# Making layer 3's masks on VectorE in the last two graphs, with the whole instruction order searched anew

## The chip, the cores and the metric

The kernel runs on one NeuronCore of a Trainium2 chip. A core has five engines that run side by side, each in the order in which its instructions were issued: TensorE (PE in the profile, with PEld for its weight loads), VectorE (DVE), ScalarE (ACT), GpSimd (POOL), and SyncE (SP), which here only issues DMAs. The metric is the device time of one execution in microseconds (us), the median over several executions. Everything is in fp32, except the masks of layer 3, which are int8.

## The reference

Four graph layers in a row are applied to each of B = 16 graphs of N = 1024 nodes with D = 128 features. `adj` is a 1024 x 1024 matrix per graph, with about 1.5% of its entries and the diagonal above zero. Each layer adds its output to `x`.

```
# before every layer: h = max(layernorm(x), 0);   x = x + layer(h)
layer 0, three times: h = h @ W + b;  n = h / |h|;  h = (adj * (n n^T)) @ h;  relu but for the last
layer 1: y = relu(((1 + eps) h + adj^T h) @ W1 + b1) @ W2 + b2, masked by node
layer 2: h = h @ W;  attn = softmax(where(adj > 0, tanh(s1_i + s2_j), -1e15));  attn @ h
layer 3: h = h @ W^T + b;  e = (h A) h^T;  e = e + e^T
         att = softmax(where(adj > 0, e, 0), axis=1) * adj
         h' = relu(att @ h);  three sigmoid gates of [x, h'];  o * tanh(sigmoid(i h' + f x))
```

The part that changes is `where(adj > 0, e, 0)` in layer 3: it needs a 0/1 mask of `adj > 0`.

## The kernel before, in words

A graph is held as eight row blocks of 128 nodes. `turn` brings `adj` in transposed, as eight tiles `adjT` of 128 x 1024 (`aT[j]`); layers 0, 2 and 3 use them. Layer 1 loads `adj` once more as it is (`adjL`).

Layers 0 and 3 need a symmetric 1024 x 1024 product. The class `Square` computes the blocks on and above the diagonal by matmul (tile `sq`, L789). The blocks below are mirrors: in the graphs from 1 to B-3 half of them take a way over HBM (`above`, `by_hbm`, `got`), in the first and the last two graphs all of them are turned by TensorE (L799) from a copy that ScalarE makes of the upper blocks (`keep`, L821). `accumulate` (L851) and `accumulate_nodes` (L862) hold the matmuls that sum over the eight rows.

Layer 3 runs over the rows j = 0 to 7. For each row:

1. the mask: ScalarE takes `Sign` of `aT[j]` into an int8 tile (L1249) and `Relu` of that in place (L1251). It needs only `adjT`, so it can be made long before the row; there are five mask buffers.
2. VectorE multiplies mask and product and keeps the row maximum (L1260, twice 512 columns, with a small read of the accumulator each), and a small reduction joins the two maxima (`top`, L1281).
3. ScalarE takes the exponential with its sum (L1292), VectorE the reciprocal (`sum`, L1306) and the product with `aT[j]` (L1301, twice 512). In the last two graphs GpSimd makes that product for four of the odd rows (L1297).
4. ScalarE scales a block of h (`hs`, L1310), and TensorE accumulates (L851).

Layer 2 has for each row a tanh (L1174) and an exp (L1178) on ScalarE, a masked product on VectorE (L1182) and the accumulation (L862). A layer norm ends with `hn` (L727 on VectorE, L734 on ScalarE); its turned copy `hnT`, and layer 3's `gT` and `h3T`, leave PSUM by ScalarE (L651).

The order of all instructions, DMAs too, is fixed while the kernel is built. The class `Plan` collects every operation with an estimated duration, reads and writes. `order` is a list scheduler: it takes, of the operations that can start on the engine that is free first, the one with the lowest rank. The rank is the due time of the graph, less the estimated work behind the operation, less a lead from the table `LEADS`. A key of `LEADS` names layer, engine and tile, and may end in an edge: ` <0` and ` <1` for the first two graphs, ` >1` and ` >0` for the last but one and the last; inner graphs have none. So a lead moves one kind of operation earlier or later against all others. `KINDS` says for each kind of tile which pool it takes buffers from, how many may be held in all and how many of these by graphs younger than the oldest unfinished one. `PERIOD` and `LAST` set the due times. Up to three graphs are in work at once.

```
o.rank = (self.deadline(o.batch) - o.tail - lead, o.seq)
...
"chunk": ("big", 11, 4)          # tile kind: (pool, most in all, most of younger graphs)
```

[...]

Of the kernel before, what the change touches and what calls it, by code (L numbers as in the profile page):

```python
# [11 lines left out]
AF = mybir.ActivationFunctionType  # L12
ALU = mybir.AluOpType
# [211 lines left out]
def tile_adj_preln(  # L225
# [40 lines left out]
    FLAGS = set("CabcdkxhyzTGmrHW")  # L266
# [61 lines left out]
    for load_it in first:  # L328
# [13 lines left out]
        "adjT": ("adjT", 16, 16), "adjL": ("adjL", 5, 5), "x": ("x", 3, 3), "w4": ("big", 9, 10),  # L342
        "chunk": ("big", 11, 4), "above": ("above", 2, 1), "got": ("got", 1, 1), "ps": ("bank", 6, 8),
        "acc": ("bank", 8, 8), "small": ("small", 8, 9), "row": ("row", 3, 2), "hbm": ("hbm", 3, 3),
        "hrow": ("hrow", 1, 2), "mask": ("mask", 5, 5), "dot": ("dot", 8, 5),
    }
    PERIOD, LAST, AHEAD, WINDOW = 59, 45.5, 2, 0.05

    LEADS = {
        "T DMA raw": 123, "T PE raw": -181.5, "T ACT adjT": 61.5, "T DVE su": 140.5, "x DMA x": -64.5,  # L350
        "0 DVE st": -1445.5, "0 DVE mv": -195, "0 POOL rstd": -141.5, "0 DVE nb": -665.5, "0 DVE hn": -152,
        "0 ACT hn": -103.5, "0 PE ps": -501, "0 ACT hT": -310, "00 PE psP": 544.5, "00 DVE h": -430.5,
        "00 PE ps": -551, "00 ACT hTn": -805, "00 ACT sq": -172.5, "00 DVE ss": 414, "00 POOL rn": 411.5,
        "00 PE sq": 2, "00 ACT above": 104.5, "00 DVE ew": 336, "00 PE acc0": -2325.5, "00 POOL params": 20.5,
        "00 DMA params": 82.5, "00 DVE params": -360, "00 PE params": -157.5, "00 ACT hT": 355.5,
        "01 PE psP": 156.5, "01 DVE h": 139.5, "01 PE ps": 225, "01 ACT hTn": -125.5, "01 ACT sq": -32.5,
        "01 DVE ss": -67.5, "01 POOL rn": -35, "01 PE sq": 593, "01 ACT above": 635, "01 DVE ew": 275,
        "01 PE acc0": -359, "01 ACT hT": -478.5, "02 PE psP": -84.5, "02 DVE h": -107, "02 PE ps": 47.5,
        "02 ACT hTn": -775.5, "02 ACT sq": -143.5, "02 DVE ss": -254.5, "02 POOL rn": 110, "02 PE sq": 1342.5,
        "02 ACT above": 29, "02 DVE ew": -245.5, "02 PE acc0": 217.5, "02 DVE x": 285, "T DMA adjT": 560,  # L360
        "T DVE adjT": -431, "1 DVE st": -145, "1 DVE mv": 965, "1 POOL rstd": 26, "1 DVE nb": 533.5,
        "1 DVE hn": 337, "1 ACT hn": 218, "1 DVE x": 944, "1 DMA adjL": -492, "1 DVE adjL": -518.5,
        "1 PE acc1": 300.5, "1 ACT g": -18, "1 PE py": -994.5, "1 ACT y1": -259.5, "1 PE py2": -40,
        "2 DVE st": 0.5, "2 DVE mv": 798, "2 POOL rstd": 84.5, "2 DVE nb": 219, "2 DVE hn": 39.5,
        "2 ACT hn": 285, "2 PE ps": -196, "2 ACT hnT": 91.5, "2 DVE alone": -149, "2 DVE x": -82.5,
        "2 PE psP": -261.5, "2 ACT h": -7, "2 DVE hrow": -299, "2 PE pf": -86, "2 ACT hfl": 3.5,
        "2 PE pt": -280.5, "2 ACT sr": 11, "2 DMA sd": -11.5, "2 DMA s1": -14.5, "2 DVE h": 147,
        "2 ACT e2": -31.5, "2 DVE e2": 44, "2 PE acc2": 764.5, "2 DVE rden": 64.5, "3 DVE st": 146.5,
        "3 DVE mv": 86.5, "3 POOL rstd": 69.5, "3 DVE nb": 1010.5, "3 DVE hn": -14.5, "3 ACT hn": 108,
        "3 PE ps": 521, "3 ACT hnT": 308, "3 PE pg": -9.5, "3 ACT gT": 17, "3 PE psP": 420.5, "3 DVE h": 402,  # L370
        "3 ACT h3T": 139.5, "3 ACT mask": -48, "3 PE sq": 515, "3 ACT above": 311, "3 DVE e3": -455.5,
        "3 DVE top": -226, "3 ACT e3": 428.5, "3 DVE sum": -301.5, "3 ACT hs": 1350.5, "3 PE acc3": -603.5,
        "3 ACT hpT": 260.5, "3 PE psN": 363, "3 ACT hp": 80.5, "3 DVE gate": -98, "3 ACT gate": 331,
        "3 POOL z": 77.5, "3 DVE z": -1081.5, "3 ACT z": 200, "3 DMA z": -878.5, "00 DVE above": 0,
        "00 DMA by": -38, "00 DMA got": 94, "01 DVE above": 266.5, "01 DMA by": -11.5, "01 DMA got": -343.5,
        "02 DVE above": 345, "02 DMA by": -362, "02 DMA got": 262.5, "3 DVE above": 240.5, "3 DMA by": 0,
        "3 DMA got": -727, "3 POOL e3": -253, "3 POOL hp": -418, "2 PE p1": -128.5, "2 ACT s1": -60,
        "T DMA raw <0": -220, "T PE raw <0": 37, "T ACT adjT <0": 8, "T DVE su <0": 268, "x DMA x <0": 168,
        "0 DVE st <0": -20, "0 DVE mv <0": -925.5, "0 POOL rstd <0": -219, "0 DVE nb <0": -16.5,
        "0 DVE hn <0": -172.5, "0 ACT hn <0": -463, "0 PE ps <0": 280.5, "0 ACT hT <0": 245.5,  # L380
        "00 PE psP <0": 16, "00 DVE h <0": 79, "00 PE ps <0": -40.5, "00 ACT hTn <0": 110.5,
        "00 ACT sq <0": 231, "00 DVE ss <0": -47, "00 POOL rn <0": 246.5, "00 PE sq <0": 67,
        "00 ACT above <0": 319.5, "00 DVE ew <0": -499.5, "00 PE acc0 <0": -127, "00 POOL params <0": -154,
        "00 DMA params <0": -52.5, "00 DVE params <0": -1.5, "00 PE params <0": 147.5, "00 ACT hT <0": -7.5,
        "01 PE psP <0": 245, "01 DVE h <0": 321.5, "01 PE ps <0": -35, "01 ACT hTn <0": 50.5,
        "01 ACT sq <0": 207.5, "01 DVE ss <0": -82, "01 POOL rn <0": -229.5, "01 PE sq <0": 1050.5,
        "01 ACT above <0": -44.5, "01 DVE ew <0": -183.5, "01 PE acc0 <0": 692, "01 ACT hT <0": -89,
        "02 PE psP <0": -136, "02 DVE h <0": -203, "02 PE ps <0": 0, "02 ACT hTn <0": -39.5,
        "02 ACT sq <0": -79.5, "02 DVE ss <0": 1, "02 POOL rn <0": -25, "02 PE sq <0": 207.5,
        "02 ACT above <0": 674.5, "02 DVE ew <0": -3.5, "02 PE acc0 <0": -198, "02 DVE x <0": 615.5,  # L390
        "T DMA adjT <1": -827, "T DVE adjT <1": -472, "T ACT adjT <1": 461, "1 DVE st <0": -232,
        "1 DVE mv <0": -265.5, "1 POOL rstd <0": 0, "1 DVE nb <0": -67, "1 DVE hn <0": 133, "1 ACT hn <0": 0,
        "1 DVE x <0": 402, "1 DMA adjL <0": -1226, "1 DVE adjL <0": 170.5, "1 PE acc1 <0": 827,
        "1 ACT g <0": 322, "1 PE py <0": 155, "1 ACT y1 <0": 102.5, "1 PE py2 <0": 178.5, "2 DVE st <0": 471,
        "2 DVE mv <0": -86.5, "2 POOL rstd <0": 0, "2 DVE nb <0": 79, "2 DVE hn <0": -357,
        "2 ACT hn <0": 108.5, "2 PE ps <0": -41, "2 ACT hnT <0": 53.5, "2 DVE alone <0": -173, "2 DVE x <0": 0,
        "2 PE psP <0": 565.5, "2 ACT h <0": 127.5, "2 DVE hrow <0": 0, "2 PE pf <0": 404.5,
        "2 ACT hfl <0": -458.5, "2 PE pt <0": 29, "2 ACT sr <0": -4, "2 DMA sd <0": -177.5,
        "2 DMA s1 <0": -231.5, "2 DVE h <0": 148.5, "2 ACT e2 <0": -217, "2 DVE e2 <0": -334,
        "2 PE acc2 <0": -70, "2 DVE rden <0": -231.5, "3 DVE st <0": -264.5, "3 DVE mv <0": 112.5,  # L400
        "3 POOL rstd <0": 41.5, "3 DVE nb <0": 379.5, "3 DVE hn <0": 33.5, "3 ACT hn <0": 62.5,
        "3 PE ps <0": 28.5, "3 ACT hnT <0": 391, "3 PE pg <0": -257.5, "3 ACT gT <0": 304, "3 PE psP <0": 17,
        "3 DVE h <0": -134, "3 ACT h3T <0": 43, "3 ACT mask <0": -116, "3 PE sq <0": 137.5,
        "3 ACT above <0": 274.5, "3 DVE e3 <0": 0, "3 DVE top <0": -269, "3 ACT e3 <0": -190,
        "3 DVE sum <0": -266, "3 ACT hs <0": 119, "3 PE acc3 <0": -253.5, "3 ACT hpT <0": 52,
        "3 PE psN <0": 42, "3 ACT hp <0": 114.5, "3 DVE gate <0": -477, "3 ACT gate <0": 224,
        "3 POOL z <0": -168.5, "3 DVE z <0": 115, "3 ACT z <0": -372, "3 DMA z <0": -268, "x DMA x <1": -50,
        "0 DVE st <1": 6.5, "0 DVE mv <1": -91.5, "0 POOL rstd <1": -321.5, "0 DVE nb <1": 0,
        "0 DVE hn <1": -14, "0 ACT hn <1": 0, "0 PE ps <1": -84, "0 ACT hT <1": 489.5, "00 PE psP <1": 458,
        "00 DVE h <1": -3.5, "00 PE ps <1": -85, "00 ACT hTn <1": -11.5, "00 ACT sq <1": 89,  # L410
        "00 DVE ss <1": 304, "00 POOL rn <1": 571.5, "00 PE sq <1": -0.5, "00 ACT above <1": 133.5,
        "00 DVE ew <1": -82.5, "00 DVE above <1": 306.5, "00 PE acc0 <1": -216, "00 DMA by <1": -110.5,
        "00 DMA got <1": -25, "00 ACT hT <1": 0, "01 PE psP <1": -27, "01 DVE h <1": 266, "01 PE ps <1": -257,
# [1120 lines left out]
```

## Time and profile before

| what | value |
|---|---|
| median of 3 runs | 2431.18 us (2430.99 to 2432.51) |
| the profiled execution's own time | 2431.62 us |
| its span, first to last instruction | 2429.9 us |
| busy PE, DVE, ACT, POOL | 2393.4, 1979.3, 1504.5, 246.7 us |
| matmul records | 11905 |
| masks L1249 and L1251 | 128 each, mean 1056 and 1052 ns |

The profile is one execution. Busy time is given per engine; a wait is put down to what released the engine last. A busy PE includes modelled ends of its matmuls, so the idle time of PE is a lower bound of what it lost. PEclk is the share of full speed that was granted to TensorE's clock.

### The profile page before, as it was taken

Reading aid. Unit: us, or ns where it says so; the run is one execution under the profiler, and the core shown is the slowest. Engines: PE = TensorE matmul, PEld = TensorE weight load, DVE = VectorE, ACT = ScalarE, POOL = GpSimd, SP = SyncE. Lnnn points to the kernel's source line nnn. Section 1 sums busy time; section 2 is a strip of 40 time slices with the busy share of each in tenths; the row PEclk is TensorE's granted clock in tenths of the full one; section 3 lists DMA queues with packets and bytes.
Section 4 is the critical chain, followed back from the end, with each engine's and each line's share of the span. In section 5 each row is a group of like instructions: output and inputs, shape, how many; then the busy total and the mean of one; then the engine's idle time right before and its main releaser. Section 6 shows DMA issues by size and latency. Waiting matters only on the chain.

```text
span 2429.9 us, 35227 instructions
## 1 busy us (share of the span) xinstructions
PE 2393.4 (98%) x11905; PEld 1588.7 (65%) x11905; DVE 1979.3 (81%) x5513; ACT 1504.5 (62%) x2661; POOL 246.7 (10%) x168
## 2 busy tenths in 40 slices
PE   8999999999999999999999999999999999999987
PEld 5568566675766757576675766757666575765764
DVE  6658889887888988889887888878889887895765
ACT  7316856656575666666656576566656656673587
POOL 3000010110101010010100101110010100000112
PEclk9999999999999999999999999999999999999989
DMA  9232939568393874929658394874929638072100
GB/s 192 71 101 52 165 67 175 124 99 170 71 175 95 137 149 82 179 61 162 142 88 165 69 173 114 107 168 78 189 68 150 150 66 148 27 105 70 44 1 18
DMA packets 1103541, 271.31 MB, mean 112 GB/s; under 512 B 937224, under 2 KB 1084816, under 8 KB 1103360
## 3 DMA queue, kind: packets, MB, share of 16 engines
q1 hardware_dynamic: 1083200, 258.35, 58.8%
q10 hardware_dynamic: 19264, 9.70, 1.4%
q8 instruction: 94, 1.54, 0.3%
q0 software_dynamic: 896, 1.01, 0.3%
q14 instruction: 87, 0.71, 0.1%
HBM read 206.00 MB, written 62.98 MB: 111 GB/s over the span
## 4 chain that ended last, share of the span: by engine, by line
PE 92%; SPq 2%; DVE 2%; DMA 2%; ACT 2%; issue 0%; POOLq 0%; POOL 0%; DVEq 0%; ACTq 0%
PE acc L851 34%; PE sq L789 19%; PE acc L862 18%; PE psP L629 5%; PE sq L799 4%; PE py L1080 2%; PE py L639 2%; PE ps_hTn L598 2%; SPq L938 2%; PE psN L629 1%; PE pg L639 1%; PE ps_hnT L598 1%; DMA by_hbm<-above 1%; DMA got<-by_hbm 1%; PE ps_hT L598 1%; SPq L842 0%
## 5 line engine op out<-in xcount | busy, mean ns | idle before, releaser
L1018 DVE SCALAR_TENSOR_TENSOR ew<-sq,rn,adjT 128x512 f32<-128x512 f32 x612 | 435.4, 739 | 83.3 <-ACT above L821 57.3
L851 PE MATMUL acc<-ew,h 128*128 128x512 f32 x1024 | 475.4, 593 | 0.1
L789 PE MATMUL sq<-hTn 128*128 128x512 f32 (+3 forms) x1152 | 433.1, 489 | 0.7 <-DVE ew L1018 0.5
L821 ACT COPY above<-sq 128x256 f32<-128x256 f32 (+3 forms) x432 | 167.0, 392 | 386.6 <-PE sq L799 223.6
L789 PEld LDWEIGHTS sq<-hTn 128*128 128x128 f32 x1152 | 196.6, 191 | 147.4 <-issue 89.0
L851 PEld LDWEIGHTS acc<-ew,h 128*128 128x128 f32 x1024 | 180.2, 190 | 166.0 <-issue 139.5
L862 PEld LDWEIGHTS acc<-h,ew 128*128 128x128 f32 x2048 | 241.0, 192 | 22.5 <-issue 9.2
L862 PE MATMUL acc<-h,ew 128*128 128x128 f32 x2048 | 250.7, 275 | 0.4 <-DVE ew L1018 0.3
L851 PE MATMUL acc<-e,hs 128*128 128x512 f32 x512 | 241.0, 601 | 5.7 <-ACT hs L1310 3.2
L862 PEld LDWEIGHTS acc<-h,e 128*128 128x128 f32 x2048 | 234.0, 193 | 12.7 <-issue 9.9
L862 PE MATMUL acc<-h,e 128*128 128x129 f32 x2048 | 235.1, 276 | 5.2 <-DVE e L1182 5.2
L851 PE MATMUL acc<-adjL,hn 128*128 128x512 f32 x512 | 233.0, 593 | 0.4 <-ACT hn L755 0.4
L591 POOL TENSOR_TENSOR rstd<-ve,mhalf 128x8 f32<-128x8 f32 x64 | 105.4, 1648 | 1104.6 <-DVE ve L710 1040.1
L799 PEld LDWEIGHTS sq<-ident,above 128*128 128x128 f32 x960 | 125.9, 141 | 113.8 <-issue 90.2
L949 ACT ACTIVATE adjT<-adjT 128x1024 f32<-128x1024 f32 x120 | 126.6, 1055 | 101.8 <-DVE adjT L946 96.7
L799 PE MATMUL sq<-ident,above 128*128 128x128 f32 x960 | 175.2, 273 | 0.3 <-DVE ew L1018 0.3
L1182 DVE SCALAR_TENSOR_TENSOR e<-adjT,e 128x512 f32<-128x512 f32 x256 | 160.1, 686 | 16.2 <-ACT e L1178 16.2
L1301 DVE TENSOR_TENSOR e<-e,adjT 128x512 f32<-128x512 f32 x248 | 164.3, 691 | 3.1 <-ACT e L1292 3.0
L811 DVE STREAM_TRANSPOSE above<-sq 128x512 f32<-128x512 f32 x208 | 144.8, 705 | 23.3 <-PE sq L789 22.4
L946 DVE STREAM_TRANSPOSE adjT<-adjT 128x1024 f32<-128x1024 f32 x120 | 144.1, 1220 | 19.7 <-DMA adjT<-in_adj_dram 18.7
L851 PEld LDWEIGHTS acc<-adjL,hn 128*128 128x128 f32 x512 | 93.2, 190 | 101.1 <-issue 87.4
L851 PEld LDWEIGHTS acc<-e,hs 128*128 128x128 f32 x512 | 91.0, 192 | 93.9 <-issue 79.3
(160 smaller groups left out, 3737.1 us busy)
## 6 DMA issues: line engine op xcount, KB each, us to landing
adjL<-in_adj_dram SPq DMA_DIRECT2D x128, 512.0 KB, 5.1
adjT<-in_adj_dram SPq DMA_DIRECT2D x480, 128.0 KB, 4.1
by_hbm<-above SPq DMA_DIRECT2D x104, 512.0 KB, 4.2
got<-by_hbm SPq DMA_DIRECT2D x416, 128.0 KB, 3.8
s<-sd SPq DMA_DIRECT2D x15, 512.0 KB, 3.7
out_dram<-z ACTq DMA_DIRECT2D x15, 512.0 KB, 3.5
x<-in_x_dram SPq DMA_DIRECT2D x13, 512.0 KB, 5.0
raw<-in_adj_dram SPq DMA_DIRECT2D x8, 512.0 KB, 7.6
```

The lines of the kernel that those rows point to most:

```text
L629: nc.tensor.matmul(dst.t[:, (c - lo) * n : (c - lo + 1) * n], cols(srcT.t, c), w, start=True, stop=True)
L789: lambda: nc.tensor.matmul(dst.t[:, (first - lo) * P :], cols(leftT.t, j), span(rightT.t, first, hi), start=True, stop=True),
L799: nc.tensor.transpose(cols(dst.t, r), cols(above.t, p), ident)
L811: lambda: nc.vector.transpose(span(above.t, p, p + 4), read.t),
L821: lambda: nc.scalar.copy(span(above.t, p, p + hi - first), read.t[:, (first - lo) * P :]),
L851: lambda s=s, lo=lo, hi=hi: nc.tensor.matmul(acc[s].t, cols(h.t, at, w), span(ew.t, lo, hi), start=(j == 0), stop=(j == NB - 1)),
L862: nc.tensor.matmul(a.t[:, (c - lo) * n : (c - lo + 1) * n], cols(ew.t, c), h.t[:, at * w : at * w + n], start=(j == 0 and c == lo), stop=( ...
L946: dve(V(N), [t], [t], lambda t=t: nc.vector.transpose(t.t, t.t), True)
L949: lambda t=t, c=c: nc.scalar.activation(t.t, t.t, AF.Copy, accum_out=su.t[:, c : c + 1]),
L1018: lambda view=view, ew=ew, rn=rn, j=j, lo=lo, hi=hi: nc.vector.scalar_tensor_tensor(by_block(span(ew.t, lo, hi), D, 4), view(), rn.t[:, j ...
L1182: lambda e=e, j=j, lo=lo, hi=hi: nc.vector.scalar_tensor_tensor(span(e.t, lo, hi), span(aT[j].t, lo, hi), 0.0, span(e.t, lo, hi), op0=ALU. ...
L1301: lambda e=e, j=j, lo=lo, hi=hi: nc.vector.tensor_mul(span(e.t, lo, hi), span(e.t, lo, hi), span(aT[j].t, lo, hi)),
```

## The change

A flag `M` is added. With it, in the graphs B-2 and B-1, the two ScalarE instructions of a mask become one VectorE instruction, `tensor_scalar` with `is_gt` against 0, from `aT[j]` (fp32) into the int8 mask. It is planned at 0.68 us[...]. The other 14 graphs keep the ScalarE masks. The branch for a flag `g` is added too, but that flag is not set.

Besides this, nearly all of some 620 numbers in `LEADS` are others (for the inner graphs too), five rows of `KINDS` have other limits, and `LAST` goes from 45.5 to 47. These change the order of the same instructions, not the instructions.

```diff
-    FLAGS = set("CabcdkxhyzTGmrHW")
+    FLAGS = set("CabcdkxhyzTGmrHWM")
...
-        "adjT": ("adjT", 16, 16), "adjL": ("adjL", 5, 5), "x": ("x", 3, 3), "w4": ("big", 9, 10),
-        "chunk": ("big", 11, 4), "above": ("above", 2, 1), "got": ("got", 1, 1), "ps": ("bank", 6, 8),
-        "acc": ("bank", 8, 8), "small": ("small", 8, 9), "row": ("row", 3, 2), "hbm": ("hbm", 3, 3),
-        "hrow": ("hrow", 1, 2), "mask": ("mask", 5, 5), "dot": ("dot", 8, 5),
+        "adjT": ("adjT", 16, 16), "adjL": ("adjL", 5, 5), "x": ("x", 3, 3), "w4": ("big", 9, 11),
+        "chunk": ("big", 10, 4), "above": ("above", 2, 1), "got": ("got", 1, 1), "ps": ("bank", 8, 8),
+        "acc": ("bank", 8, 6), "small": ("small", 8, 15), "row": ("row", 3, 2), "hbm": ("hbm", 3, 3),
+        "hrow": ("hrow", 1, 2), "mask": ("mask", 5, 5), "dot": ("dot", 8, 6),
...
-    PERIOD, LAST, AHEAD, WINDOW = 59, 45.5, 2, 0.05
+    PERIOD, LAST, AHEAD, WINDOW = 59, 47, 2, 0.05
...
-        "2 PE psP": -261.5, "2 ACT h": -7, "2 DVE hrow": -299, "2 PE pf": -86, "2 ACT hfl": 3.5,
+        "2 PE psP": -2328.5, "2 ACT h": -84.5, "2 DVE hrow": -74, "2 PE pf": -2468, "2 ACT hfl": -232,
...
-                act(
-                    S(N), [aT[j]], [mask],
-                    lambda mask=mask, j=j: nc.scalar.activation(mask.t, aT[j].t, AF.Sign),
-                )
-                act(S(N), [mask], [mask], lambda mask=mask: nc.scalar.activation(mask.t, mask.t, AF.Relu))
+                if "M" in FLAGS and b >= B - 2:
+                    dve(
+                        0.68, [aT[j]], [mask],
+                        lambda mask=mask, j=j: nc.vector.tensor_scalar(mask.t, aT[j].t, 0.0, None, op0=ALU.is_gt), True,
+                    )
+                elif "g" in FLAGS:
...
+                else:
+                    act(
+                        S(N), [aT[j]], [mask],
+                        lambda mask=mask, j=j: nc.scalar.activation(mask.t, aT[j].t, AF.Sign),
+                    )
+                    act(S(N), [mask], [mask], lambda mask=mask: nc.scalar.activation(mask.t, mask.t, AF.Relu))
```

## The prediction

> **What bounds the kernel now.** First the page: busy time, and the span in 40 slices.
>
> ```profile
> PE 2393.4 (98%) x11905; PEld 1588.7 (65%) x11905; DVE 1979.3 (81%) x5513; ACT 1504.5 (62%) x2661; POOL 246.7 (10%) x168
> ...
> PE   8999999999999999999999999999999999999987
> ...
> ACT  7316856656575666666656576566656656673587
> ...
> PEclk9999999999999999999999999999999999999989
> ```
>
> PE is the bound over the whole: 98%, with full slices everywhere but at the ends. ACT, 62% as a mean, has its fullest stretch in the last slices (5, 8, 7), where PE is not full. So I cut the span by windows (columns: window, length, busy us of PE, PEld, DVE, ACT, POOL with counts, granted clock, DMA share, GB/s).
>
> ```profile
> 300.00:1900.00 1600.00, 1599.69 (x7930) 1058.18 (x7929) 1370.16 (x3786) 1008.06 (x1764) 143.41 (x86) 1.00 0.70 126
> ...
> 2320.00:2346.00 26.00, 19.74 (x133) 17.39 (x132) 14.57 (x36) 25.45 (x38) 1.10 (x1) 0.87 0.00 1
> 2346.00:2380.00 34.00, 30.01 (x141) 18.72 (x141) 25.50 (x89) 28.80 (x47) 6.80 (x3) 0.90 0.00 1
> 2380.00:2400.00 20.00, 19.03 (x71) 10.10 (x69) 13.72 (x41) 19.80 (x38) 4.71 (x2) 1.00 0.00 0
> 2400.00:2419.00 19.00, 16.68 (x59) 8.95 (x58) 12.40 (x30) 12.09 (x27) 10.44 (x5) 0.91 0.00 1
> ```
>
> In the inner graphs PE idles 0.3 us in 1600: no order can gain there, and every wait newly made costs its full length. From 2320 to 2419 (the last matmul) PE idles 99 - 85.5 = 13.5 us, and its clock is lowered too: (0.13 x 26) + (0.10 x 34) + (0.09 x 19) = 8.5 us of full speed are not granted. From 2320 to 2400 ACT is busy 74.05 of 80 us, DVE 53.8, PE 68.8: **the tail is bound by ACT**. PE's waits name what it stood for (total, times, longest):
>
> ```profile
> PE acc L862 <- DVE e L1182: 5.2, 1, 5.2
> PE acc L851 <- ACT hs L1310: 3.2, 2, 2.3
> PE acc L851 <- DVE e L1301: 2.4, 2, 2.2
> ```
>
> The first is the start of the last graph's layer 2, the others are rows of layer 3, behind an exp or `hs` of ACT. What fills ACT, by group in the window 2320 to 2419 (count, then busy us, mean ns):
>
> ```profile
> L1249 ACT ACTIVATE mask<-adjT 128x1024 int8<-128x1024 f32 x11 | 11.5, 1053 | 1.4 <-DVE peak L1260 1.4
> L1251 ACT ACTIVATE mask<-mask 128x1024 int8<-128x1024 int8 x11 | 11.4, 1053 | 0.0
> ```
>
> Eleven of the last two graphs' 16 masks lie in the tail, 22.9 of ACT's 86.2 us there. They lie on the path too. The chain of waits, in order of time (start, us, what):
>
> ```profile
> 2370.87 1.06 ACT mask L1249
> 2371.93 0.50 ACT hnT L651
> 2372.43 0.94 ACT mask L1249
> 2373.38 0.95 ACT mask L1251
> 2374.32 0.94 ACT mask L1249
> 2375.27 1.89 ACT mask L1251 x2
> 2377.16 1.15 ACT gT L651 x2
> 2378.31 0.97 ACT h3T L651 x2
> ```
>
> `gT` could leave PSUM when its first matmul pair ended, about 2372.7 by the timeline; behind the masks it began at 2377.1, and the last layer 3 waited for it. All mask pieces of the chain after 2320 sum to 8.6 us (2326.25, 2327.86, the five above, 2384.60).
>
> [...] the clock falls only at the start, around PE's idle stretches in the tail, and at the end; 0.87 over 26 us is 6.8 us at half. [...] `w2f` (TENSOR_SCALAR, SBUF) 217 ns, copies from PSUM 281 to 292[...] L673's `x` takes 362 ns as a rule, but four of them took 3.24 us beside the GpSimd product that began at 2352.61.
>
> **The change, part by part.** *Removed*: 16 x (1056 + 1052) = 33.7 us of ACT, 11 x 2.11 = 23.2 in the tail. Their wait goes too: L1249 stood 5.8 us over the kernel for VectorE's reads of the old mask (L1260); now writer and reader are both VectorE, in order.
>
> *Added*: 16 DVE instructions. [...] 1.22 us, as the 1024-wide transpose L946 takes (1220 ns). I take 0.68, [...] the copy from uint8 (L1434) is at 220 ns too[...]; int8 as a target is not in the trace. Eleven in the tail: 7.5 us (13.4 at the high end). A mask waits only for `adjT`, there long before, and a free buffer. Queued behind it on DVE are products that feed exp and PE, late by 0.68 us each if the mask is placed badly. Its cover is DVE's idle time, 80 - 53.8 = 26 us before 2400: layer 2's eight rows leave 0.69 us beside each exp (L1182 waits 8.5 us there), just a mask's size. If that cover is gone, a mask is paid on layer 3's path.
>
> *The bound after it.* ACT 74.1 - 23.2 = 51 us of the 80, DVE 53.8 + 7.5 = 61 (67 at the high price), PE 68.8 less what the clock stretched, about 63. PE and DVE then stand level, so 80 us could shrink to about 65 if nothing waited; chains (norm, turn, product, exp, sum) keep part of it.
>
> *What I take for the tail.* The chain loses 8.6 us of masks and gets the same 4.3 masks (8.6 / 2.0 us of chain each) back at DVE's price, 2.9: -5.7. [...] Sum -9.1. The other view agrees: two thirds of 13.5 us idle is 9. Bounds: 13.5 + 8.5 = -22 if PE never stops; 0 if each wait is only renamed.
>
> *Moved*: everything. Matmuls, copies and DMAs are the same in number[...]. In the inner graphs each queue is covered by PE's backlog: SP's loads land in 3.8 to 5.1 us and PE never waited for one there; I cost this at 0, at most +14 (below). No gain is possible there: 0.3 us idle. At the start PE waits 7.4 us for the first `raw` DMA, which no order removes, and 2.3 us for `hT`; leads of graph 0 are new: -1, from -2.3 to +2. The `KINDS` limits have no cost but through the order. The drain after the last matmul (2418.7 to 2429.9, 11.2 us: gates on DVE and ACT, then the output DMA) has the same steps: 0.
>
> *Sum*: -9.1 - 1 = -10.1 on the profiled execution's own 2431.62 us, so 2421.5; its median lay 0.44 lower, so **2421 us**.
>
> **The rivals.** *A better packing*: the search closes nearly all tail waits, -14 to -22, about 2413. For it: ACT gets 23 us free[...]. Against it: the last graph's chain has no other graph beside it after about 2400.
>
> *The wait moves to DVE*: masks cost 1.22 us and meet GpSimd's products (2.4 us each, four in the tail)[...]. Then 4.3 x 1.22 = 5.2 us come back on the chain and, at half of each product, 4.8 more: 10.0 against the 8.6 removed. With the clock's part gone too the tail is where it was, about 2430. Against it: DVE's 26 idle us.
>
> *Slower*: the new leads cost the inner graphs. `2 PE psP` goes from -261.5 to -2328.5, so layer 2's projection is taken when PE has nothing else, and its rows follow late; or a `got` transfer (4.2 and then about 5 us in the chain of one graph) lands behind its reader. PE has no slack, so 1 us per inner graph is 13 us. It decides from 10 / 13 = 0.8 us a graph; at 1.5 us the sum is -10 + 20, 2441. Against it: the same kind of plan gave waits of 0.3 us in 1600, and these DMAs have several us in hand.
>
> *The change does nothing*: the flag acts on 16 masks and is set; it can only be that the order leaves the freed ACT unused, which is the case of 2430.
>
> **The numbers.** Forecast 0.55 (2416 to 2426), better packing 0.18, DVE takes the wait 0.17, slower 0.10. A measurement of this kernel can tell about 0.2%, 4.9 us, from no change. The first two lie past 2426.3: faster 0.73; same 0.17; slower 0.10. The range reaches down into the better packing, 2410, and up over the case of 2430 to 2433; outside are a third of the better packing (0.06) and most of the slower case (0.09).
>
> **What would show it.** Right: 112 pairs L1249/L1251 instead of 128; 16 rows of TENSOR_SCALAR on `mask` near 0.68 us; ACT in the last 100 us under 70%, DVE over 70%; fewer half-clock slices near the end; the last matmul near 2408; windows of inner graphs with PE full as before. Wrong: masks of 1.2 us; PE in the tail waiting for DVE's L1260 or L1301 as long as before; PE idle by tenths of a us in every inner graph.

## The result, and the profile after

The changed kernel takes **2414.33 us** (median of 6 runs, 2411.87 to 2416.11) against 2431.85 us (6 runs, 2430.99 to 2433.79) of the kernel before: ratio 0.9928, interval 0.9918 to 0.9939. That is 17.5 us less where 10 were forecast: inside the range, in the forecast direction, but at the size of the rival called better packing (2413). The profiled execution took 2413.47 us, its span is 2411.7. In the new kernel.py the lines after the masks stand a little lower: L1260 is now L1272, L1301 is L1313, L1297 is L1309, L851 is L852, L651 is L652, L673 is L674; the mask on VectorE is L1251.

The page of the kernel after, busy time and slices:

```profile
PE 2384.0 (99%) x11905; PEld 1586.1 (66%) x11905; DVE 1985.5 (82%) x5529; ACT 1474.7 (61%) x2629; POOL 251.1 (10%) x168
...
PE   8999999999999999999999999999999999999988
...
ACT  7326756656675666666656566565756656654566
PEclk9999999999999999999999999999999999999998
```

The work is what the change said: as many matmuls, 16 instructions more on DVE, 32 fewer on ACT. ACT's last three slices fell from 5, 8, 7 to 5, 6, 6.

Where the 17.5 us went is read best from one matmul that every graph has once at the same place of its work, the first `py<-g,w` of layer 1. The starts of these matmuls divide each execution into three stretches: the start (up to graph 0's), the inner graphs (from there to graph 15's) and the tail (from there to the last matmul). The tile `py` near the end, kernel before, then kernel after (count, duration in ns, first and last start in us):

```profile
L639 PE MATMUL py<-g,w x8: 592/592/592, 2308.2 to 2311.2; 128*128 128x512 f32 x8
```
```profile
L640 PE MATMUL py<-g,w x8: 592/592/592, 2299.7 to 2302.7; 128*128 128x512 f32 x8
```

So 8.5 us had been gained before the tail began. The three stretches for all runs of this study, in us, from one profiled execution of each (e1 to s5 are the experiments below):

| kernel | start | inner graphs | tail | last matmul |
|---|---|---|---|---|
| before | 170.13 | 2138.03 | 110.52 | 2418.68 |
| after | 164.96 | 2134.74 | 100.91 | 2400.60 |
| after, once more | 167.13 | 2134.71 | 101.30 | 2403.14 |
| e1: new order, masks on ACT | 165.89 | 2138.21 | 108.09 | 2412.20 |
| e2: old order, masks on DVE | 171.64 | 2138.96 | 110.22 | 2420.82 |
| s1: new start, then old order | 165.15 | 2136.12 | 108.83 | 2410.10 |
| s2: old order, then new tail | 170.39 | 2139.73 | 100.72 | 2410.85 |
| s4: new order to 1880, then old | 167.06 | 2135.14 | 111.30 | 2413.50 |
| s5: new start, old inner, new tail | 165.94 | 2136.82 | 98.73 | 2401.48 |
| e3: each DVE mask twice | 165.16 | 2135.02 | 106.02 | 2406.20 |
| e5: one GpSimd product later | 168.76 | 2134.72 | 100.67 | 2404.15 |
| e6, e8: PE's wait filled | 166.44, 164.56 | 2134.71, 2134.70 | 97.97, 97.97 | 2399.12, 2397.24 |
| e7: e5 and a shorter fill | 167.58 | 2134.71 | 100.31 | 2402.60 |

After minus before: start -5.2, inner -3.3, tail -9.6, sum -18.1; the drain after the last matmul stayed at 11 us. A profiled execution isn't always a typical one: that of s1, at 2423.04 us, is the fastest of its 14 (median 2426.28). The new start ranges from 164.6 to 168.8 between executions (mean of eleven 166.2), the old one from 170.1 to 171.6 (mean of three 170.7). The new order's inner graphs repeat to hundredths wherever nothing in them was edited, so they can be compared where medians can't. The tail repeats less well: the old order with the old masks took 110.52 before, 108.83 in s1 and 111.30 in s4, and these differ in TensorE's clock (see e6 and e8).

A long stretch of the inner graphs and the tail by windows, after, and then the tail before (columns as in the prediction):

```profile
300.00:1900.00 1600.00, 1600.00 (x7942) 1060.03 (x7941) 1371.41 (x3795) 1007.75 (x1765) 148.84 (x87) 1.00 0.64 127
2299.70:2400.60 100.90, 94.03 (x466) 63.59 (x465) 75.32 (x234) 71.14 (x131) 23.27 (x11) 0.95 0.00 1
```
```profile
2308.16:2418.68 110.52, 97.02 (x466) 63.76 (x465) 71.90 (x223) 91.08 (x153) 23.26 (x11) 0.92 0.00 1
```

With the same 466 matmuls, PE's idle time fell from 13.5 to 6.9 us and its busy time by 3.0. As their number is the same, the clock may have a part in those 3.0: 17.1 us of the tail ran at half clock (granted 0.50) before, 10.2 after. ACT fell from 91 to 71 us; DVE rose by only 3.4, less than the 7.7 of its eleven masks; part of the difference is that the products L1313 last 682 ns there, where L1301 took 775 (24 of them). What PE still waits for after, over the whole kernel:

```profile
PE raw L599 <- DMA raw<-in_adj_dram: 7.7, 2, 7.6
PE sq L790 <- DVE peak L1272: 4.7, 1, 4.7
PE acc L852 <- DVE ew L1019: 1.5, 2, 0.9
PE psP L630 <- ACT hnT L652: 1.4, 2, 0.7
```

The waits for the exp product, for layer 2's first row and for `hs` are gone. One of 4.7 us took their place: PE stands at 2346 to 2350.8, because the next `sq` needs a bank that VectorE's product L1272 has not read yet. What VectorE does instead, in the chain of waits (start, us, what):

```profile
2341.39 1.20 DVE mask L1251 x2
...
2343.47 4.26 DVE x L674 x8
2347.72 1.56 DVE st L700 x8
```

### The profile page after: what moved, and what is told of

It is laid out like the page before. It is cut to its first block, busy times and chain, and to the rows that moved or that the text cites. A ratio compares the mean times of both kernels' runs of the same rounds, so it can differ in the third digit from the quotient of the medians.

```text
span 2411.7 us, 35199 instructions
## 1 busy us (share of the span) xinstructions
PE 2384.0 (99%) x11905; PEld 1586.1 (66%) x11905; DVE 1985.5 (82%) x5529; ACT 1474.7 (61%) x2629; POOL 251.1 (10%) x168
## 4 chain that ended last, share of the span: by engine, by line
PE 95%; SPq 1%; DVE 1%; ACT 1%; DMA 1%; issue 0%; DVEq 0%
PE acc L852 35%; PE sq L790 20%; PE acc L863 18%; PE psP L630 6%; PE sq L800 4%; PE py L1081 2%; PE py L640 2%; PE ps_hTn L599 2%; PE psN L630 1%; PE ps_hnT L599 1%; PE pg L640 1%; SPq L939 1%; PE ps_h3T L599 1%; PE ps_hT L599 0%; ACT e L1175 0%; DVE ew L1019 0%
## 5 line engine op out<-in xcount | busy, mean ns | idle before, releaser
L852 PE MATMUL acc<-ew,h 128*128 128x512 f32 x1024 | 478.1, 593 | 1.5 <-DVE ew L1019 1.5
L822 ACT COPY above<-sq 128x384 f32<-128x384 f32 (+3 forms) x432 | 167.7, 393 | 415.9 <-PE sq L800 225.1
L852 PEld LDWEIGHTS acc<-ew,h 128*128 128x128 f32 x1024 | 180.4, 190 | 166.2 <-issue 137.3
L852 PE MATMUL acc<-e,hs 128*128 128x512 f32 x512 | 238.3, 594 | 0.0
L852 PE MATMUL acc<-adjL,hn 128*128 128x512 f32 x512 | 232.8, 592 | 0.0
L1313 DVE TENSOR_TENSOR e<-e,adjT 128x512 f32<-128x512 f32 x248 | 162.0, 682 | 3.8 <-ACT e L1304 3.7
L852 PEld LDWEIGHTS acc<-adjL,hn 128*128 128x128 f32 x512 | 93.5, 190 | 101.2 <-issue 87.7
L812 DVE STREAM_TRANSPOSE above<-sq 128x512 f32<-128x512 f32 x208 | 145.0, 706 | 15.8 <-PE sq L790 14.7
L1272 DVE CUSTOM_DVE_ANT_0 e<-mask,sq 128x512 f32<-128x512 int8 x204 | 135.5, 676 | 20.1 <-ACT above L822 12.0
```

Source lines behind the costliest of these rows:

```text
L812: lambda: nc.vector.transpose(span(above.t, p, p + 4), read.t),
L822: lambda: nc.scalar.copy(span(above.t, p, p + hi - first), read.t[:, (first - lo) * P :]),
L852: lambda s=s, lo=lo, hi=hi: nc.tensor.matmul(acc[s].t, cols(h.t, at, w), span(ew.t, lo, hi), start=(j == 0), stop=(j == NB - 1)),
L1272: lambda e=e, view=view, mask=mask, peak=peak, s=s, lo=lo, hi=hi: nc.vector.tensor_tensor_reduce(by_block(span(e.t, lo, hi), D, 4), by_blo ...
L1313: lambda e=e, j=j, lo=lo, hi=hi: nc.vector.tensor_mul(span(e.t, lo, hi), span(e.t, lo, hi), span(aT[j].t, lo, hi)),
```

## The experiments

Kernels with an order put together from both plans follow a list, which replaces the planner's choice; each instruction's own work stays. The edits are shown shortened, with their helpers left out.

### e1, the new order with the old masks

```diff
-    dve(0.68, [aT[j]], [mask], lambda: nc.vector.tensor_scalar(mask.t, aT[j].t, 0.0, None, op0=ALU.is_gt), True)
+    # at the planned place of the DVE mask:
+    nc.scalar.activation(mask.t, aT[j].t, AF.Sign); nc.scalar.activation(mask.t, mask.t, AF.Relu)
```

> The order of the changed kernel, but the 16 masks of the last two graphs made by ScalarE again (Sign and Relu at the place in the list where the VectorE mask stood). Theory A (the tail was bound by ScalarE, the masks' move frees it): ScalarE gets 11 x 2.1 = 23 us back in a tail in which it is busy 68 of 94 us, so it is full again and the end comes 8 to 12 us later than in the changed kernel: 2422 to 2427. Theory B (the new order alone makes the gain, the masks hardly matter): 2414 to 2417.

2425.57 us (2424.81 to 2427.58), ratio 0.9978 [0.9969, 0.9986]. In this order the VectorE masks are worth 11.2 us: 7.2 in the tail and 3.5 before it, nearly all between the `py` of graphs 13 and 14, where graph 14's first masks lie. In the tail PE waits 5.6 us for ACT's `hnT`: the first `hnT`, at 2362.7, stands behind both instructions of a mask (2360.7 and 2361.8), the second, at 2366.9, behind those of another (2364.3 and 2365.4) and an `hn`. The wait, and the tail by its window:

```profile
PE psP L630 <- ACT hnT L652: 5.6, 2, 2.8
2304.10:2412.20 108.10, 94.50 (x467) 63.29 (x465) 67.80 (x223) 91.85 (x153) 23.07 (x11) 0.97 0.00 1
```

### e2, the old order with the new masks

```diff
+    # graphs B-2 and B-1 only; the others keep both ScalarE instructions
+    nc.vector.tensor_scalar(mask.t, aT[j].t, 0.0, None, op0=ALU.is_gt)   # in the first of the two places
-    nc.scalar.activation(mask.t, aT[j].t, AF.Sign); nc.scalar.activation(mask.t, mask.t, AF.Relu)
```

> The order of the kernel before, but the 16 masks of the last two graphs made by VectorE, each at the place of the old Sign, the Relu left out. Theory A: ScalarE's chain loses 8.6 us of masks and gets 2.9 back from VectorE, so 5 to 7 us less than before: 2425 to 2427, with the start and the inner graphs as before. Theory B: within 1 us of before, 2431 to 2433. A third, that the masks make the whole tail gain of 9.6 us without a new order: 2422.

2432.52 us (2431.47 to 2433.74), ratio 1.0003 [0.9995, 1.0011]: **nothing**, where a gain was expected. Its tail, and what PE waited for there:

```profile
2310.60:2420.82 110.22, 95.53 (x466) 63.96 (x465) 78.15 (x234) 72.07 (x131) 23.58 (x11) 0.94 0.00 1
```
```profile
PE acc L851 <- DVE e L1311: 4.8, 3, 3.4
PE acc L862 <- DVE e L1182: 4.2, 1, 4.2
PE acc L851 <- ACT hs L1320: 2.3, 1, 2.3
PE ps_hnT L598 <- DVE hn L727: 2.0, 1, 2.0
```

ACT is freed as forecast, 91.1 to 72.1 us, and PE idles 14.7 us, no less than before (13.5). The waits keep their places, and three of the four name DVE, as before. Ahead of the product that ends the wait of 3.4 us (it starts at 2363.4) DVE makes two masks, at 2359.6 and 2361.2; a mask at 2366.7 takes 1.82 us beside a GpSimd product that began at 2365.6. In the tail masks alone gave -0.3, the order with ACT's masks -2.4, both -9.6. PE's idle time in the tail tells it more plainly: 13.5 us before, 14.7 with the masks alone, 13.6 with the order alone (e1), 6.9 with both. The order's -2.4 goes with a clock that stood at half for 6.8 us instead of 17.1. So what is gained in PE's waits needs both.

### s1 and s2, the new order in one part only

```diff
-    ordered = plan.order()
+    ordered = plan.follow(ORDER)   # s1: what the new plan has before 200 us, then the old order (ACT masks)
+                                   # s2: what the old plan has before 2300 us, then the new order (DVE masks)
```

> The changed kernel's order for what was planned in the first 200 us, then the order of before for all the rest; ScalarE masks as before. If the lead of 5.2 us that the trace of the changed kernel has after its first graph comes from the order of the start and is kept to the end: 2426 to 2427.5. If it is only an advance that a later load or wait takes back: 2430 to 2432.

> The order of before for what was planned in its first 2300 us, then the changed kernel's order; VectorE masks in the last two graphs. If tail and start are separate gains: 9 to 10 us less than before, 2421 to 2423, with the start's waits of before still there. If the tail's gain needs the 8.5 us of lead: 2426 to 2431.

s1: 2426.28 us (14 runs, 2423.04 to 2430.25), ratio 0.9978 [0.997, 0.9986], 5.5 us gained. s2: 2423.23 (2422.98 to 2423.74), ratio 0.9965 [0.9953, 0.9978], 8.5 us gained. The two gains are separate, and together 14.0 of 17.5. Neither kernel isolates its stretch fully: the inner graphs were 1.9 us shorter in s1 than before and 1.7 longer in s2. In the start PE's waits of s1 up to 170 us are, beside those of before:

```profile
PE raw L629 <- DMA raw<-in_adj_dram: 7.3, 2, 7.1
PE acc L882 <- DVE ew L1049: 2.0, 2, 1.0
```
```profile
PE raw L598 <- DMA raw<-in_adj_dram: 7.4, 2, 7.2
PE psP L629 <- ACT hT L651: 2.3, 1, 2.3
```

The wait for `hT` is gone, and with it a half-clock stretch of 3.4 us that followed it in the kernel before (68.3 to 71.7). Over the first 170 us PE's idle time falls from 11.2 to 9.3 us; with at most 1.7 for the clock, an estimate from half of those 3.4 us, that is up to 3.6 of the 5.0 by which the start is shorter. The rest shows in no view. The half-clock stretch isn't gone for good: in e5, which has the same new start, a wait of 2.1 us for `ew` was followed by 6.8 us of it (69.9 to 76.7), and its start of 168.76 is the longest of the new ones.

### s4 and s5, the inner graphs

```diff
-    ordered = plan.order()
+    ordered = plan.follow(ORDER)   # s4: new plan before 1880 us, then the old order (ACT masks)
+                                   # s5: new start as in s1, old order to 2300 us, then the new tail (DVE masks)
```

> As s1, but the changed kernel's order is kept for what was planned in the first 1880 us; then the order of before, ScalarE masks. The trace of the changed kernel gains another 2.2 us from its second to its thirteenth graph. If that is real: 2 us less than s1, 2423.5 to 2425. If it is the scatter of one execution: as s1, 2426 to 2427.

> VectorE masks; the changed kernel's order for what it plans before 200 us, then the order before for what that plans before 2300 us, then the changed order for the tail. Theory A, the gain is start plus tail and the inner graphs give 2 to 3 us of it: 2416 to 2419 us (the two separate gains, 5.5 and 8.5 us, sum to 14.0, so 2417.8). Theory B, start and tail together are the whole gain, and the inner graphs' new order gives nothing: the same as the changed kernel within 1 us, 2413 to 2415.

s4: 2425.06 us (2421.66 to 2426.45), ratio 0.997 [0.9959, 0.9981]: 1.2 below s1, which the scatter of the start covers. By the table its inner graphs are 1.0 shorter than s1's and its tail 2.5 longer. s5: 2416.55 (2414.06 to 2417.84), ratio 0.9935 [0.9922, 0.9947], 2.8 above the changed kernel's 2413.78 on the same chip; its inner graphs are 2.1 longer. The median fits theory A, but the intervals overlap, and its tail was 2.2 to 2.6 shorter for another reason (below). Of those 2.1 us some belong to the masks, not the order: with the old order there, s5's inner graphs are 0.7 longer than s1's, which has ScalarE's masks, and e2's 0.9 longer than before. So the new order of the inner graphs gives some 1 to 2 us. Of the inner -3.3, 1.9 are there already in s1 (2136.12 against 2138.03), with the old order after the new start; why, the runs don't show.

### e3, each mask on VectorE made twice

```diff
-    lambda: nc.vector.tensor_scalar(mask.t, aT[j].t, 0.0, None, op0=ALU.is_gt)
+    lambda: [nc.vector.tensor_scalar(mask.t, aT[j].t, 0.0, None, op0=ALU.is_gt) for _ in range(2)]
```

> The changed kernel with each of the 16 VectorE masks made twice, one after the other. If the mask's price is covered by VectorE's idle time, as the prediction said (cover named: 26 us): at most 2 us more than the changed kernel, 2414 to 2416.5. If VectorE now sets the tail's pace: the eleven extra masks of the tail cost 0.61 us each from start to start, up to 6.7 us: 2418 to 2421.

2420.24 us (2418.56 to 2423.45), ratio 0.9954 [0.994, 0.9967], 5.9 above after. The tail, and all masks that VectorE makes in this kernel (ns least/median/most):

```profile
2300.18:2406.20 106.02, 95.04 (x466) 62.97 (x465) 86.21 (x245) 71.03 (x131) 23.52 (x11) 0.95 0.00 1
L1251 DVE TENSOR_SCALAR mask<-adjT x32: 675/692/2857, 2027.9 to 2381.2; 128x1024 int8<-128x1024 f32 x32
```

DVE has 10.9 us more of work and PE starts its last matmul 5.1 later into the tail. The 11 masks added would be 7.7 us at the 704 ns that a mask takes in the tail of the kernel after. But two of them, at 2358.6 and 2368.7, met a GpSimd product and took 2.86 and 2.73 us instead of some 0.69: these two meetings are 4.2 us of the added work. DVE still stands idle for 20 of 106 us, so idle time in the sum did not cover what was added. What the extra masks would have cost without the two meetings, e3 doesn't show.

### e5, one GpSimd product out of VectorE's way

```diff
# ORDER: one op moved in GpSimd's queue, the product e<-e,adjT of graph B-2, row 3
-    product, ..., rstd of the last graph
+    rstd of the last graph, product
```

> The changed kernel with one GpSimd product of the last graph but one (L1309, at 2344.53 in its trace) put behind the last graph's rstd in GpSimd's queue, so that it no longer runs beside VectorE's eight x instructions (L674). [...] they take 2.1 us less, TensorE's wait of 4.7 us for VectorE gets shorter by that, 1.5 to 3 us less in all: 2411.5 to 2413. If the product, now late, makes the accumulation wait as long, or the stretch has another cause: 2414 to 2416.

2413.58 us (2412.47 to 2417.07), ratio 0.9927 [0.9914, 0.9939]: as after. The rows `x` that come ahead of L1272, in the kernel after and then in e5 (ns least/median/most):

```profile
L674 DVE SCALAR_TENSOR_TENSOR x<-o,rden,x x8: 337/344/2442, 2343.4 to 2347.4; 128x128 f32<-128x128 f32 x8
```
```profile
L705 DVE SCALAR_TENSOR_TENSOR x<-o,rden,x x8: 344/346/351, 2347.2 to 2349.1; 128x128 f32<-128x128 f32 x8
```

In the kernel after one `x` took 2442 ns instead of 344: it overlaps the GpSimd product that runs from 2344.53 for 2.53 us. In e5 that row is back at 346 and PE's wait for L1272 is 2.6 instead of 4.7 us; but PE then waits 1.8 us for the last graph's `hn` from DVE, so the tail is only 0.2 shorter. The product, now at 2353.44 for 2.34 us, meets another row of VectorE: `nb`, a small step of the layer norm that stands ahead of `hn`. Its line in the kernel after, then in e5 (start, us, what):

```profile
2351.88 0.16 DVE L719 SCALAR_TENSOR_TENSOR nb<-mv,rstd 128x8 f32<-128x8 f32 x1
2353.56 2.25 DVE L750 SCALAR_TENSOR_TENSOR nb<-mv,rstd 128x8 f32<-128x8 f32 x1
```

So e5 moved the collision one link further down the chain and did not remove it. What a tail without it would take, no run shows.

### e6 and e8, PE's wait filled

```diff
+    # after row 1's accumulate of graph B-2; zero is 128 x 128 of zeros, so the sum stays
+    for _ in range(5):
+        nc.tensor.matmul(acc[1].t, zero, span(aT[7].t, 0, 4), start=False, stop=False)
```

> The changed kernel with five more matmuls (zero weights, 512 columns, added to an accumulator, which they leave as it is) in TensorE's queue where it waits 4.7 us for VectorE; 4.3 us of work at full clock. If the idle time causes the half-clock stretch of 10.2 us behind it (2349.3 to 2359.6): that stretch goes, and the end comes 3 to 5 us earlier though TensorE does more: 2409.5 to 2411.5. If the lowered clock costs nothing because TensorE waits for others there anyway: 2413.5 to 2415. If the fill is in the way: above 2415.

> The changed kernel with five matmuls with zero weights in TensorE's 4.7 us wait, once more, now on the same chip as the changed kernel. Theory A, the clock's half-speed stretch of 10.2 us costs time: 2411.5 to 2412.7, about 2 us under the changed kernel's median of this call. Theory B, the first result was scatter of the start: within 0.5 us of the changed kernel.

e6: 2412.44 us (2411.98 to 2412.69), ratio 0.992 [0.9906, 0.9933]. e8, the same kernel on another chip: 2412.00 (2410.12 to 2412.29), ratio 0.9917 [0.9904, 0.9931]. On e8's chip the changed kernel ran at 2413.78 (2412.62 to 2416.09), 0.9928 [0.9915, 0.994]:

> The changed kernel itself, for a comparison on one chip with the three others of this call. Both theories: 2412 to 2416 us, ratio to the kernel before 0.992 to 0.994.

The stretch around the wait, in the kernel after and in e8 (the third column from the end is the clock):

```profile
2340.00:2360.00 20.00, 14.66 (x62) 10.41 (x61) 17.98 (x68) 9.88 (x21) 7.72 (x4) 0.74 0.00 1
```
```profile
2340.00:2360.00 20.00, 18.76 (x89) 11.66 (x88) 19.77 (x72) 11.34 (x24) 7.30 (x4) 1.00 0.00 1
```

The tail's 10.2 us at half clock are gone, and the tail is 97.97 us, twice, against 100.91 and 101.30: **2.9 to 3.3 us less with a clock that stays up** (granted 1.00 over the tail in e8, 0.95 in the kernel after), though TensorE does 4.4 us more of work. The `sq` behind the wait starts 51.1 us into the tail in both, so the gain comes after it. By the medians the fill gave 1.8 us (e8 against the changed kernel on its chip), less than the tails differ and short of the 3 to 5 us expected for e6; between executions the start alone scatters by more than that. s5 agrees without a fill: the same wait of 4.7 us, but the records show only 3.4 us at half, and its tail is 98.73.

```profile
2340.00:2360.00 20.00, 14.66 (x86) 11.43 (x85) 19.50 (x70) 11.01 (x24) 7.47 (x4) 0.91 0.01 1
```

In s5 the half-clock stretch begins as the stop ends (2354.0), in the kernel after within it (2349.3, the stop ends at 2350.8). So stops of the same length went with 10.2 and with 3.4 us at half; why, no run shows. The old order says the same: before, s1 and s4 have the same three longest stops in the tail (5.2, 2.2 and 2.3 us), but 17.1, 10.2 and 17.1 us at half, and s1's tail is 1.7 and 2.5 us the shorter. The filled kernel is the fastest of this study, by the tail and by both medians; the intervals of its ratio still overlap that of after.

### e7, the product later and a shorter fill

```diff
# ORDER as in e5, and the fill of e6 with range(3)
```

> The changed kernel with both of the tail's edits: one GpSimd product (graph B-2, row 3) issued behind the last graph's rstd, and three matmuls with zero weights, which add nothing to the sum, put into TensorE's wait (2.6 us long then). Theory A, what is left in the tail's wait is partly TensorE's clock and partly VectorE's collision with GpSimd, and the two gains add: 2409.5 to 2411.5 us. Theory B, the wait only moves to the next link (hn of the last graph's layer 3), as it did with the product moved alone: 2412 to 2414.

2414.54 us (2413.43 to 2415.46), ratio 0.9928 [0.9914, 0.9942]: no gain. PE's wait for `hn` (2.0 us) was followed by 6.8 us at half clock, and the tail is 100.31. That wait stands behind the same collision as in e5 (`nb` took 2248 ns), so one of the two gains was not there to be added; the fill sat in an earlier wait and could not cover it.

## Why the prediction was right and wrong

**The tail: the right sum by a wrong step.** -9.1 forecast, -9.6 measured. The step "the chain loses 8.6 us of masks and gets 2.9 back: -5.7" took the masks' length on the chain as gain. e2 made exactly that exchange in the old order and its tail moved by -0.3: PE's waits stayed, two of the masks now standing on VectorE ahead of one of them. Of the orders that were run, only the one planned for the free ACT turned the exchange into time. In that order the chain of the tail holds 1.2 us of masks, two pieces at 2341, not the 4.3 pieces carried over from before. The sum came out near by luck: the clock gave less than forecast (below), and the waits more.

**The clock.** The other -3.4 of the forecast was the author's estimate for the clock: 6.8 us less at half speed. The records show 17.1 us at half in the tail before and 10.2 after, so 6.8 less before rounding, as estimated. But e6 and e8 price them lower: 10.2 us at half cost 2.9 to 3.3, not half of their length, 5.1. In part that is because 1.5 us of them lie in the stop itself; the rest isn't shown. By that price 6.8 us are worth about 2, so some 7.6 of the 9.6 are left for the waits, where 5.7 were forecast. What sets the length of a half-clock stretch, no run shows: the same stop of 4.7 us went with 10.2 us in the kernel after and 3.4 in s5, and shorter ones were followed by such stretches too, e7's wait of 2.0 us by 6.8 and one of 2.3 us at the start of the kernel before (to 67.7) by 3.4 (as far as the records tell, since matmul ends are modelled).

**The mask's price.** 0.68 us was the author's estimate, which no row of the kernel before showed; 684 ns were measured, and the high bound of 1.22 fell. Against the 217 ns of `w2f`, 128 columns wide, that is 467 ns for 896 more columns:

```profile
L1251 DVE TENSOR_SCALAR mask<-adjT x16: 672/684/907, 2027.7 to 2374.3; 128x1024 int8<-128x1024 f32 x16
```

**Its cover was wrong.** "DVE's 26 idle us before 2400" was a sum over 80 us, and idle time counts only where a mask may lie. In e3 the added work, two collisions included, put the last matmul 5.1 us later into the tail, with 20 us idle left.

**The start was mis-sized**: -1 forecast; -5.2 in the first pair of profiles, -4.5 by the means of all, and -5.5 by s1's median, which holds some of the inner graphs' gain too. The range given to that term, -2.3 to +2, took only the named waits as what could be gained.

**"No gain is possible there", said of the inner graphs, was wrong by 3.3.** It was read from 0.3 idle us in 1600. After shows 1600.00 busy in the same window, and yet the inner graphs are 3.3 shorter with the same matmuls. Busy ends are modelled: a short stop can be covered by the record of the matmul before it.

**The rivals.** The wait did move to DVE, as the second rival had it, with a GpSimd product beside it (2442 ns for one `x`); but masks cost 0.68, and in the new order the move gained 7.2 us in the tail (e1). That rival took half of each product as lost. In the profile before, the "four of them" at 3.24 us are three of 0.35 and one of 2.46: that row ended at 2355.29, the product beside it at 2355.14. In the kernel after, the `x` row of 2442 ns began at 2344.76 and ended at 2347.2, just after the product's end at 2347.06. In the old order (e2) this rival's outcome is what came. The slower case, the inner graphs losing 0.8 us each, didn't come: they gained. Better packing named the total but not the place: in the tail 22 us was its end and 9.6 came.

**Signs.** 112 pairs of ACT masks: yes. ACT under 70% near the end: 69.4% of the last 100 us, at the line (70.5% of the tail's 100.9). DVE over 70%: 76.2% (74.6% of the tail). Last matmul near 2408: 2400.6, by start and inner graphs.

## What to carry to other kernels

Work moved off a crowded engine can give nothing by itself when other pieces are as late; test the move and the order apart before you credit either. Divide both traces at one and the same instruction and compare the stretches: that showed 8.5 us in places where busy time and waits seemed to have little or none to give, and it repeats to hundredths in the inner graphs when the whole run scatters by microseconds. When an edit takes a collision or a wait away, look at the next link of the chain: in e5 the collision had only moved. Where TensorE stood for 4.7 us, matmuls that add zero kept its clock up (e8: granted 1.00 from 2340 to 2360, where the kernel after has 0.74); behind a stop of 2.0 us that they did not cover it still fell (e7: 0.87 in the same stretch).

## What the runs showed of the hardware that was not expected

- A stop of 4.7 us went with 10.2 us at half clock in the kernel after and 3.4 in s5; with 4.4 us of zero matmuls in it there was none, and the tail was 2.9 to 3.3 us shorter.
- Beside a GpSimd product of 2.53 us a single VectorE row took 2442 ns instead of 344, though neither needs the other's data; in e5, beside a product of 2.34 us, one took 2.25 us instead of 161 ns.
- From graph 0's `py` to graph 15's the same order took 2134.70 to 2134.74 us in six profiled executions that differed by 4.2 us at the start.
